# Layer 0 FFN: selecting the top 128 from quarters instead of halves, and narrow products in four column groups

## The chip, the cores and the metric

The kernel runs on one core of a Trainium2 chip. The metric is the time of one execution on the device in microseconds (us), from the first to the last instruction and what lies around them; of several runs the median counts. A profile of one execution gives the start and duration of each instruction on each engine: TensorE (PE; its weight loads PEld), VectorE (DVE), ScalarE (ACT), GpSimd (POOL) and SyncE (SP).

## What is computed

The reference is a network of four layers over x of 4 x 512 x 128 float32 values. Each layer is a feed-forward part (FFN), an attention and the same FFN again, each added to x. The change touches the FFN of layer 0 alone, which runs twice, before and after layer 0's attention:

```
def _L0_ffn_ref(x, input_patterns, process_input_weights, process_values, output_input_weights, output_patterns):
    k_input = max(n_input // 8, 64)        # 1024 // 8 = 128
    k_process = max(n_process // 8, 32)    # 512 // 8 = 64
    k_output = max(n_output // 8, 64)      # 1024 // 8 = 128
    input_acts = gelu(jnp.einsum('bsd,nd->bsn', x, input_patterns))
    input_acts_seq = input_acts.mean(axis=1)
    top_input_acts, top_input_idx = jax.lax.top_k(input_acts_seq, k_input)
    brow = jnp.arange(B)[:, None]
    input_repr = jnp.zeros((B, n_input), x.dtype).at[brow, top_input_idx].set(top_input_acts)
    process_acts = gelu(jnp.einsum('bn,pn->bp', input_repr, process_input_weights))
    top_process_acts, top_process_idx = jax.lax.top_k(process_acts, k_process)
    selected_process_values = process_values[top_process_idx]
    process_weights = jax.nn.softmax(top_process_acts, axis=-1)
    aggregated_value = jnp.einsum('bk,bkd->bd', process_weights, selected_process_values)
    output_acts_seq = gelu(jnp.einsum('bd,od->bo', aggregated_value, output_input_weights))
    top_output_acts, top_output_idx = jax.lax.top_k(output_acts_seq, k_output)
    selected_output_patterns = output_patterns[top_output_idx]
    out_per_seq = jnp.einsum('bk,bkm->bm', top_output_acts, selected_output_patterns)
    return jnp.broadcast_to(out_per_seq[:, None, :], (B, S, d_model))
```

The caller adds half of it: `x = x + 0.5 * _L0_ffn_ref(_layernorm(x), ...)`. There are four sequences, so each selection takes the 128 largest of 1024 numbers for each of four rows.

## The kernel before, in words

All of x stays in SBUF, and so do the weights of layer 0 (tile `w0`, one column block for each matrix) and the constants (tile `cst`, among them `selb`, four matrices of which the b-th copies row b to all 128 partitions). The layers follow one another. Inside a stage a scheduler orders the instructions of each engine, but for those that `mm_in_order` and `transpose_in_order` pin to the program's order. Engines wait for one another by semaphores. Products are recorded in the profile under the lines of their helpers: `mm` is L158, `transpose` L161, `mm_in_order` L164; they are told apart by the tiles that they write.

`l0_ffn` (from L329, called at L1822 and L1824) works in this order, and each step needs the one before:

1. For each of four sequences, eight products of input patterns with the normalized x (tile `pa`), each followed by a Gelu on ScalarE that also sums over the positions, into one column of `acc` (L346). POOL sets `acc` and `agg` to zero at the start (L334), because only 4 of 32 columns are used.
2. `acc` is turned by four transposes into rows, `ra`: 64 partitions of 512, the first half of the 1024 numbers on partitions 0 to 3, the second on 32 to 35. VectorE scales one half (L407), ScalarE the other (L408). `vals` is the same by neuron (L410).
3. `largest` finds the 128th largest number of each row. It runs 16 rounds on both halves at once. MAX8 (L365) takes the eight largest of each partition in falling order; MATCH_REPLACE8 (L367, with a short load of the eight values) writes a very low number over them. So each half gets a list of 128 in falling order. One list is read backwards (L370), and the maximum of the two lists position by position (L371) holds the 128 largest of both; their minimum (L373) is the limit. The limit is spread over the partitions by a small transpose (L374 to L378), and comparisons with `vals`, with a rule for ties by place (L380 to L399), give the numbers that are kept, all others zero (L401).
4. These, 128 x 4 in each of eight chunks, are the stationary side of eight products with `piw` that add up in one bank, `pp` (4 partitions x 512), then Gelu (L418).
5. The top 64 of 512 on four partitions (L424 and L425), softmax (L429 to L434), transposes (`pt_w`) and products (`pg`) to `agg` (L444).
6. Two products with `oiw` write the output row in two halves of 512 (`po0`), each followed by a Gelu into `oa` (L450). `by_neuron` transposes `oa` (L354), and `largest` runs again, on `oa`.
7. Eight products with `op` add up in `po1` (4 x 128), VectorE copies them to `o4` (L457), four products with `selb` spread row b over all partitions (`pb`), and four VectorE operations add to x (L464).

A float32 product is two instructions (passes) on TensorE. PSUM has banks with the tags "s" (4), "t" (2) and "m" (2). After the second call the tile of `w0` is loaded with the weights of layer 3 (L1826).

Of the kernel before, what the change touches and what calls it, by code (L numbers as in the profile page):

```python
# [103 lines left out]
def tile_macaron(ctx, tc, x_in, const_in, vec_in, w0_in, ws_in, ws3_in, w2f_in, w3_in, out):  # L104
# [223 lines left out]

    def l0_ffn(tag):  # L329
        with pool(tag) as sb:  # L330
            acc = sb.tile([P, 4, 2, 32], F32, name="acc")
            agg = sb.tile([64, 32], F32, name="agg")
            for padded in (acc, agg):
                nc.gpsimd.memset(padded, 0.0)  # L334
            ra = sb.tile([64, 512], F32, name="ra")
            oa = sb.tile([64, 512], F32, name="oa")
            halves = (slice(0, 32), slice(32, 64))
            finish_chains()
            ip = W0(w0, "ip")
            for b in range(B):  # L340
                begin_sequence(b, True)
                for c in range(8):
# [3 lines left out]
                    nc.scalar.activation(ga, pa, AF.Gelu, accum_out=acc[:, c % 4, c // 4, b : b + 1])  # L346

            def by_neuron(row, name):
# [3 lines left out]
                for c in range(4):  # L352
                    transpose(pt[:, ts(c, 64)], row[:, ts(c, P)])
                nc.vector.tensor_copy(  # L354
                    r.rearrange("p (h c) b -> p c h b", h=2), pt[:, :256].rearrange("p (c h b) -> p c h b", c=4, h=2)[:, :, :, :B]
# [3 lines left out]
            def largest(row, vals, name):  # L359

                w = sb.tile([64, 512], F32, tag="w512", name=f"w_{name}")
                order = sb.tile([64, P], F32, tag="order", name="order")
                for i in range(P // 8):
                    m8, src = order[:, ts(i, 8)], w if i else row
                    nc.vector.max(m8, src)  # L365
                    if i < P // 8 - 1:
                        nc.vector.match_replace(w, m8, src, GONE)  # L367
                turned = sb.tile([B, P], F32, tag="turned", name="turned")
                a = order[32 : 32 + B, P - 1 : P]
                nc.vector.tensor_copy(turned, bass.AP(a.tensor, a.offset, [list(a.ap[0]), [-1, P]]))  # L370
                nc.vector.tensor_tensor(turned, turned, order[:B, :], ALU.max)  # L371
# [28 lines left out]
                r = sb.tile([P, 8, B], F32, tag="kept", name=name, bufs=2)  # L400
                nc.vector.tensor_mul(r, above, vals)  # L401
                return r

            pt = bank("t", "pt_a")
            for c in range(4):
                transpose(pt[:64, ts(c, P)], acc[:, c, :, :].rearrange("p h b -> p (h b)"))
            nc.vector.tensor_scalar_mul(ra[halves[0]], pt[halves[0]], 1.0 / S)  # L407
            nc.scalar.activation(ra[halves[1]], pt[halves[1]], AF.Copy, scale=1.0 / S)  # L408
# [45 lines left out]
            for c in range(8):  # L454
                mm(po[:B, :D], oT[:, c, :], op[:, c, :], c == 0, c == 7)
# [1537 lines left out]
```

## Time and profile before

| What | Value |
|---|---|
| Median of three runs | 2940.64 us |
| Lowest and highest | 2930.02 and 2940.65 us |
| The profiled execution's own time | 2936.27 us |
| Its span, first to last instruction | 2934.6 us |
| Mean granted TensorE clock | 0.864 |
| First call of `l0_ffn`, up to its last addition to x | 0 to 144.3 us |
| Second call, from the normalization to its last addition | 287.7 to 417.1 us |
| DVE busy in 48 to 142 us | 65.1 of 94.0 us |
| DVE busy in 320 to 415 us | 65.4 of 95.0 us |

In a row of the timeline stand the start and the duration in us, the engine, the line, the operation, the tile written and the tiles read, partitions x elements of each, and how many are merged in that row; brackets hold the idle time before it and what ended that. In a table of stretches each engine's busy us stand with the number of its instructions in parentheses, then the granted TensorE clock, the share of DMA and its GB/s.

### The profile page before, as it was taken

Reading aid. Unit: us, or ns where it says so; the run is one execution under the profiler, and the core shown is the slowest. Engines: PE = TensorE matmul, PEld = TensorE weight load, DVE = VectorE, ACT = ScalarE, POOL = GpSimd, SP = SyncE. Lnnn points to the kernel's source line nnn. Section 1 sums busy time; section 2 is a strip of 40 time slices with the busy share of each in tenths; the row PEclk is TensorE's granted clock in tenths of the full one; section 3 lists DMA queues with packets and bytes.
Section 4 is the critical chain, followed back from the end, with each engine's and each line's share of the span. In section 5 each row is a group of like instructions: output and inputs, shape, how many; then the busy total and the mean of one; then the engine's idle time right before and its main releaser. Section 6 shows DMA issues by size and latency. Waiting matters only on the chain.

```text
span 2934.6 us, 46900 instructions
## 1 busy us (share of the span) xinstructions
PE 2274.4 (78%) x17558; PEld 1179.6 (40%) x17558; DVE 1808.6 (62%) x4776; ACT 1246.5 (42%) x2682; POOL 913.9 (31%) x1700
## 2 busy tenths in 40 slices
PE   4277528888678998958577678988689999689987
PEld 2145213333333333338456545555322222355553
DVE  4656476676576676454564477777356564777763
ACT  3044303433332433314232266776224444467763
POOL 1012012332122222202322387775200000677661
PEclk8588758999887999768777789999779999899998
DMA  3042010000000000008105410000000000100000
GB/s 133 0 152 81 0 58 1 1 1 1 1 1 1 1 1 4 4 7 290 36 13 189 143 30 21 21 21 12 1 1 1 1 1 1 26 23 19 21 21 11
DMA packets 33771, 99.12 MB, mean 34 GB/s; under 512 B 6184, under 2 KB 12072, under 8 KB 33032
## 3 DMA queue, kind: packets, MB, share of 16 engines
q1 hardware_dynamic: 30616, 88.03, 9.2%
q0 software_dynamic: 2496, 5.12, 0.8%
q8 instruction: 138, 2.26, 0.3%
q10 hardware_dynamic: 432, 2.98, 0.3%
q14 instruction: 89, 0.73, 0.1%
HBM read 66.88 MB, written 14.55 MB: 28 GB/s over the span
## 4 chain that ended last, share of the span: by engine, by line
PE 51%; DVE 22%; ACT 10%; POOL 9%; issue 6%; DMA 2%; SPq 0%; POOLq 0%; DVEq 0%; ACTq 0%
PE pk_at L164 10%; PE po_at L164 6%; ACT PT L787 4%; PE pa L164 3%; PE pag L164 3%; PE po L164 3%; PE pe L164 3%; PE p_qk L164 2%; POOL t L1603 2%; PE pg L164 2%; DVE t L1599 2%; PE pv L164 2%; DVE t L1596 2%; DVE y L997 2%; PE pq_at L164 2%
## 5 line engine op out<-in xcount | busy, mean ns | idle before, releaser
L787 ACT ACTIVATE PT<-pk_at 128x1024 f32<-128x1024 f32 (+3 forms) x384 | 311.1, 810 | 554.6 <-PE pq_at L164 478.1
L164 PE MATMUL pk_at<-qx,km 32*128 32x512 f32 (+3 forms) x1536 | 372.2, 562 | 62.3 <-ACT PT L787 57.3
L164 PE MATMUL po_at<-PT,vh 128*32 128x512 f32 (+3 forms) x1536 | 335.1, 519 | 3.1 <-POOL PT L790 2.8
L757 DVE CUSTOM_DVE_ANT_0 s<-pq_at,cst 128x384 f32<-128x384 f32 (+3 forms) x512 | 248.6, 485 | 100.8 <-PE pq_at L164 89.5
L1548 ACT ACTIVATE s<-s,nm,rn 128x128 f32<-128x128 f32 x512 | 245.5, 482 | 2.3 <-DVE nm L1654 2.0
L790 POOL TENSOR_SCALAR_AFFINE_SELECT PT<-PT 128x256 f32<-128x256 f32 x256 | 107.6, 422 | 422.9 <-ACT PT L787 422.8
L164 PE MATMUL pq_at<-km,qT 32*128 32x384 f32 (+3 forms) x1024 | 225.9, 530 | 14.1 <-DVE nm L757 7.7
L164 PEld LDWEIGHTS pk_at<-qx,km 32*128 32x128 f32 x1536 | 121.0, 191 | 271.9 <-ACT PT L787 209.0
L752 DVE TENSOR_REDUCE nm<-pq_at 128x2 f32<-128x1024 f32 x128 | 156.2, 1225 | 104.8 <-PE pq_at L164 104.0
L1603 POOL TENSOR_TENSOR t<-t,t 128x1024 f32<-128x1024 f32 x64 | 151.5, 2367 | 134.7 <-DVE t L1599 134.4
L161 PE MATMUL pt_y<-ident,y 128*128 128x128 f32 x224 | 54.6, 375 | 156.9 <-DVE y L214 117.9
L164 PE MATMUL pq_at<-km,t 32*128 32x512 f32 x512 | 149.6, 690 | 7.0 <-DVE nm L752 4.8
L164 PE MATMUL p_qk<-w,hT 128*128 128x512 f32 x256 | 144.0, 691 | 10.8 <-DVE t L1599 9.0
L164 PEld LDWEIGHTS po_at<-PT,vh 128*32 128x32 f32 x1536 | 56.0, 110 | 222.7 <-issue 148.2
L161 PE MATMUL pt<-ident,s 128*128 128x128 f32 x640 | 93.3, 293 | 65.4 <-POOL s L1666 40.4
L241 ACT COPY yT<-pt_y 128x512 f32<-128x512 f32 x56 | 32.8, 585 | 258.1 <-PE pt_y L161 258.1
L1666 POOL TENSOR_TENSOR s<-s,sm 128x1024 f32<-128x1024 f32 x64 | 121.5, 1898 | 49.1 <-DVE sm L1665 41.0
L1596 DVE TENSOR_TENSOR t<-p_qk,w 128x1024 f32<-128x1024 f32 x64 | 78.3, 1223 | 71.4 <-ACT sq L1548 71.1
L1548 ACT ACTIVATE sq<-p_qk 128x1024 f32<-128x1024 f32 x64 | 65.6, 1024 | 128.3 <-PE p_qk L164 72.7
L161 PEld LDWEIGHTS pt<-ident,s 128*128 128x128 f32 x640 | 78.6, 151 | 97.6 <-POOL s L1666 51.3
L161 PEld LDWEIGHTS pt_y<-ident,y 128*128 128x128 f32 x224 | 34.6, 171 | 188.1 <-issue 112.1
L1290 DVE SCALAR_TENSOR_TENSOR hT<-pa,w,sg 128x128 f32<-128x128 f32 x184 | 51.8, 345 | 85.1 <-ACT sg L1289 64.0
(424 smaller groups left out, 5197.0 us busy)
## 6 DMA issues: line engine op xcount, KB each, us to landing
w<-in_w2f_dram SPq DMA_DIRECT2D x46, 836.0 KB, 5.8
vb<-v SPq DMA_DIRECT2D x112, 128.0 KB, 2.2
skew<-qe SPq DMA_DIRECT2D x16, 512.0 KB, 3.0
rel<-skew SPq DMA_DIRECT2D x64, 128.0 KB, 3.5
w<-in_w_dram SPq DMA_DIRECT2D x1, 4147.0 KB, 12.4
w<-in_w_dram SPq DMA_DIRECT2D x1, 3200.0 KB
od<-o SPq DMA_DIRECT2D x46, 64.0 KB, 4.9
yd<-y SPq DMA_DIRECT2D x8, 256.0 KB, 2.3
```

Source lines behind the costliest of these rows:

```text
L161: return nc.tensor.transpose(dst, src, ident[: src.shape[0], : src.shape[0]])
L164: tc.keep_in_program_order(nc.tensor.matmul(dst, lhsT=lhsT, rhs=rhs, start=start, stop=stop))
L752: nc.vector.tensor_reduce(to, pq.rearrange("p (i n) -> p i n", i=2), AX.X, ALU.max)
L757: nc.vector.tensor_tensor_reduce(s[:, :nk], pq[:, i * 512 : i * 512 + nk], causal[:, S - nk :], 1.0, -BIG, ALU.add, ALU.max, nm[:, qt, at ...
L787: by_order(nc.scalar.activation(PT[:, :, q0:], pk[:, :, q0:], AF.Exp, scale=SC8))
L790: nc.gpsimd.affine_select(d, d, pattern=[[0, 2], [1, P]], base=0, channel_multiplier=-1, compare_op=ALU.is_ge, fill=0.0)
L997: nc.vector.scalar_tensor_tensor(yt, pe[e // 4][:, ts(e % 4, D)], st["g"][:, t, e : e + 1], yt, ALU.mult, ALU.add)
L1548: tc.keep_in_program_order(nc.scalar.activation(*args, **kw))
L1596: nc.vector.tensor_mul(by_head(t1), by_head(p3), over(tab[:, 0]))
L1599: nc.vector.tensor_mul(by_head(t2[:, :, a]), by_head(p3[:, :, z]), over(tab[:, 1, :, a]))
L1603: nc.gpsimd.tensor_add(t1, t1, t2)
L1666: nc.gpsimd.tensor_mul(s, s, bcast(sm, P))
```

## The change

`largest` works on quarters. `acc` is laid out so that two full transposes give 128 partitions of 256: quarter q of sequence b on partition 32 q + b. The 16 rounds run on 128 x 256. After them lie four sorted lists of 128 for each sequence. A new helper, `larger`, does what L370 and L371 did: one list read backwards, and the maximum with the other. It is called first for 64 partitions (quarters 2 and 3 against 0 and 1). What it leaves are the 128 largest of each pair, no longer in falling order but rising and falling at most once, so seven stages of maximum and minimum over halves, quarters and so on put them in order again, between two tiles `two`. Then `larger` is called for four rows, as before.

The result goes into one of two tiles `kept`, 32 columns a chunk of which four are used, zeroed once on POOL. In the products with `piw` and `op` chunk c goes to the 32-partition strip c % 4 of PSUM: four strips with two chunks each. For `piw` the strips are copied to SBUF in two parts and added by one product with the first columns of `selb`, which now has its ones in all four strips; for `op` the four products with `selb` add them. The output row is four products of 256 columns, one a strip, and one Gelu of 128 x 256. No load is added; the constant has the same size.

The diff, cut to its core:

```diff
@@ -326,15 +326,18 @@
     def l0_ffn(tag):
         with pool(tag) as sb:
-            acc = sb.tile([P, 4, 2, 32], F32, name="acc")
+            acc = sb.tile([P, 2, 4, 32], F32, name="acc")
             agg = sb.tile([64, 32], F32, name="agg")
-            for padded in (acc, agg):
+            kept = [sb.tile([P, 8, 32], F32, name=f"kept{i}") for i in range(2)]
+            for padded in (acc, agg, *kept):
                 nc.gpsimd.memset(padded, 0.0)
-            ra = sb.tile([64, 512], F32, name="ra")
-            oa = sb.tile([64, 512], F32, name="oa")
-            halves = (slice(0, 32), slice(32, 64))
+            ra = sb.tile([P, 256], F32, name="ra")
+            oa = sb.tile([P, 256], F32, name="oa")
+            selb = const("selb")
             finish_chains()
             ip = W0(w0, "ip")
             for b in range(B):
@@ -343,32 +346,43 @@
                     pa = bank("s", "pa")
                     mm_in_order(pa, ip[:, ts(c, P)], yT[:, b, :])
                     ga = sb.tile([P, S], F32, tag="ga", name="ga", bufs=2)
-                    nc.scalar.activation(ga, pa, AF.Gelu, accum_out=acc[:, c % 4, c // 4, b : b + 1])
+                    nc.scalar.activation(ga, pa, AF.Gelu, accum_out=acc[:, c % 2, c // 2, b : b + 1])
 
             def by_neuron(row, name):
 
                 r = sb.tile([P, 8, B], F32, tag="by_n", name=name, bufs=2)
                 pt = bank("t", "pt_c")
-                for c in range(4):
-                    transpose(pt[:, ts(c, 64)], row[:, ts(c, P)])
+                for c in range(2):
+                    transpose(pt[:, ts(c, P)], row[:, ts(c, P)])
                 nc.vector.tensor_copy(
-                    r.rearrange("p (h c) b -> p c h b", h=2), pt[:, :256].rearrange("p (c h b) -> p c h b", c=4, h=2)[:, :, :, :B]
+                    r.rearrange("p (q c) b -> p c q b", q=4),
+                    pt[:, :256].rearrange("p (c q b) -> p c q b", c=2, q=4)[:, :, :, :B],
                 )
                 return r
 
-            def largest(row, vals, name):
-
-                w = sb.tile([64, 512], F32, tag="w512", name=f"w_{name}")
-                order = sb.tile([64, P], F32, tag="order", name="order")
+            def larger(dst, lists, n, at):
+
+                a = lists[at : at + n, P - 1 : P]
+                nc.vector.tensor_copy(dst, bass.AP(a.tensor, a.offset, [list(a.ap[0]), [-1, P]]))
+                nc.vector.tensor_tensor(dst, dst, lists[:n, :], ALU.max)
+
+            def largest(row, vals, r):
+
+                w = sb.tile([P, 256], F32, tag="w256", name="w256")
+                order = sb.tile([P, P], F32, tag="order", name="order")
                 for i in range(P // 8):
                     m8, src = order[:, ts(i, 8)], w if i else row
                     nc.vector.max(m8, src)
                     if i < P // 8 - 1:
                         nc.vector.match_replace(w, m8, src, GONE)
+                two = [sb.tile([64, P], F32, tag=f"two{i}", name="two") for i in range(2)]
+                larger(two[0], order, 64, 64)
+                for i in range(7):
+                    halves = [t.rearrange("p (n i k) -> p n i k", i=2, k=64 >> i) for t in (two[i % 2], two[1 - i % 2])]
+                    for to, op in enumerate((ALU.max, ALU.min)):
+                        nc.vector.tensor_tensor(halves[1][:, :, to, :], halves[0][:, :, 0, :], halves[0][:, :, 1, :], op)
                 turned = sb.tile([B, P], F32, tag="turned", name="turned")
-                a = order[32 : 32 + B, P - 1 : P]
-                nc.vector.tensor_copy(turned, bass.AP(a.tensor, a.offset, [list(a.ap[0]), [-1, P]]))
-                nc.vector.tensor_tensor(turned, turned, order[:B, :], ALU.max)
+                larger(turned, two[1], B, 32)
                 limit = sb.tile([B, 1], F32, tag="limit", name="limit")
                 nc.vector.tensor_reduce(limit, turned, AX.X, ALU.min)
                 nc.vector.tensor_copy(turned, limit.to_broadcast([B, P]))
@@ -397,23 +411,25 @@
                     equal, place[:, : 8 * B].rearrange("p (c b) -> p c b", b=B), float(P), equal, ALU.is_le, ALU.mult
                 )
                 nc.vector.tensor_add(above, above, equal)
-                r = sb.tile([P, 8, B], F32, tag="kept", name=name, bufs=2)
-                nc.vector.tensor_mul(r, above, vals)
-                return r
+                nc.vector.tensor_mul(r[:, :, :B], above, vals)
 
             pt = bank("t", "pt_a")
-            for c in range(4):
-                transpose(pt[:64, ts(c, P)], acc[:, c, :, :].rearrange("p h b -> p (h b)"))
-            nc.vector.tensor_scalar_mul(ra[halves[0]], pt[halves[0]], 1.0 / S)
-            nc.scalar.activation(ra[halves[1]], pt[halves[1]], AF.Copy, scale=1.0 / S)
+            for c in range(2):
+                transpose(pt[:, ts(c, P)], acc[:, c, :, :].rearrange("p q b -> p (q b)"))
+            nc.vector.tensor_scalar_mul(ra, pt[:, :256], 1.0 / S)
             vals = sb.tile([P, 8, B], F32, tag="by_n", name="vals", bufs=2)
-            nc.vector.tensor_scalar_mul(vals.rearrange("p (h c) b -> p c h b", h=2), acc[:, :, :, :B], 1.0 / S)
-            reprT = largest(ra, vals, "reprT")
-
-            pp = bank("m", "pp")
+            nc.vector.tensor_scalar_mul(vals.rearrange("p (q c) b -> p c q b", q=4), acc[:, :, :, :B], 1.0 / S)
+            largest(ra, vals, kept[0])
+
+            p4 = bank("m", "pp4")
             piw = W0(w0, "piw").rearrange("p (c n) -> p c n", n=512)
             for c in range(8):
-                mm(pp[:B, :], reprT[:, c, :], piw[:, c, :], c == 0, c == 7)
+                mm(p4[ts(c % 4, 32), :], kept[0][:, c, :], piw[:, c, :], c < 4, c >= 4)
+            pq = sb.tile([P, 512], F32, name="pq4")
+            nc.vector.tensor_copy(pq[:, 0:256], p4[:, 0:256])
+            nc.vector.tensor_copy(pq[:, 256:512], p4[:, 256:512])
+            pp = bank("m", "pp")
+            mm(pp[:B, :], selb.rearrange("p (b n) -> p b n", n=P)[:, :, 0], pq)
             pa = sb.tile([B, 512], F32, name="pact")
             nc.scalar.activation(pa, pp[:B, :], AF.Gelu)
 
@@ -444,21 +460,20 @@
             nc.vector.tensor_copy(agg[:, :B], pg[:64, :B])
 
             oiw = W0(w0, "oiw")
-            for half, at in enumerate(halves):
-                po = bank("m", "po0")
-                mm(po[at, :], agg, oiw[:64, ts(half, 512)])
-                nc.scalar.activation(oa[at], po[at, :], AF.Gelu)
-            oT = largest(oa, by_neuron(oa, "out"), "oT")
+            po = bank("m", "po0")
+            for q in range(4):
+                mm(po[ts(q, 32), :256], agg, oiw[:64, ts(q, 256)])
+            nc.scalar.activation(oa, po[:, :256], AF.Gelu)
+            largest(oa, by_neuron(oa, "out"), kept[1])
             po = bank("m", "po1")
             op = W0(w0, "op").rearrange("p (c n) -> p c n", n=D)
             for c in range(8):
-                mm(po[:B, :D], oT[:, c, :], op[:, c, :], c == 0, c == 7)
-            o4 = sb.tile([B, D], F32, name="o4")
-            nc.vector.tensor_copy(o4, po[:B, :D])
+                mm(po[ts(c % 4, 32), :D], kept[1][:, c, :], op[:, c, :], c < 4, c >= 4)
+            o4 = sb.tile([P, D], F32, name="o4")
+            nc.vector.tensor_copy(o4, po[:, :D])
             pb = bank("m", "pb")
-            selb = const("selb")
             for b in range(B):
-                mm(pb[:, ts(b, D)], selb[:B, ts(b, P)], o4)
+                mm(pb[:, ts(b, D)], selb[:, ts(b, P)], o4)
             for b in range(B):
                 xb = x[:, ts(b, TB), :]
                 nc.vector.scalar_tensor_tensor(xb, rows(pb[:, ts(b, D)], TB), 0.5, xb, ALU.mult, ALU.add)
@@ -1861,8 +1876,8 @@
     f8 = np.arange(128) // HD
     m3 = np.where(k128 < 64, k128 >= i64, k128 - 64 <= i64)
     m3f = m3 & ((p[:, None] >= 64) | (k128 >= 64))
-    selb = np.zeros((B, B, P), f)
-    selb[np.arange(B), np.arange(B), :] = 1.0
+    selb = np.zeros((4, 32, B, P), f)
+    selb[:, np.arange(B), np.arange(B), :] = 1.0
     perm = np.zeros((P, P), f)
     perm[p, p ^ 1] = 1.0
     return CONST.pack({
@@ -1877,7 +1892,7 @@
         "pm4": (p[:, None] // 32 == f8[None, :] % 4).astype(f),
         "perm": perm, "kmask": ((p[:, None] % 32) // HD == np.arange(4)[None, :]).astype(f),
         "kmax": -((p[:, None] % 32) == HD * (np.arange(4)[None, :] ^ 1)).astype(f),
-        "rev": np.broadcast_to(8.0 - np.arange(8), (P, 8)), "selb": selb,
+        "rev": np.broadcast_to(8.0 - np.arange(8), (P, 8)), "selb": selb.reshape(P, B * P),
         "iota": np.broadcast_to(np.arange(128), (P, 128)), "row1": p[:, None] * NT + np.arange(NT)[None, :] + 1,
         "lower8": np.broadcast_to(np.tri(8, 8, -1)[None], (P, 8, 8)),
     })
```

## The prediction

> **What bounds the kernel now.** I read the page first, for the span and the chain of work that ended last.
>
> ```profile
> span 2934.6 us, 46900 instructions
> PE 2274.4 (78%) x17558; PEld 1179.6 (40%) x17558; DVE 1808.6 (62%) x4776; ACT 1246.5 (42%) x2682; POOL 913.9 (31%) x1700
> ...
> PE 51%; DVE 22%; ACT 10%; POOL 9%; issue 6%; DMA 2%; SPq 0%; POOLq 0%; DVEq 0%; ACTq 0%
> ```
>
> TensorE bounds the kernel as a whole, but this is an average over stages. The change touches two stages only, the two calls of the layer 0 FFN (some 0 to 144 and 290 to 417 us), so I then asked for the busy time in the four stretches in which `largest` takes its top 128.
>
> ```profile
> core 0: us, PE busy (x) PEld busy (x) DVE busy (x) ACT busy (x) POOL busy (x), PEclk, DMA share, GB/s
> 51.17:74.42 23.25, 0.00 (x0) 0.00 (x0) 22.16 (x47) 0.00 (x0) 0.00 (x0) 0.53 0.00 0
> 107.70:131.08 23.38, 0.68 (x4) 0.50 (x4) 22.25 (x48) 0.00 (x1) 0.00 (x0) 0.50 0.00 0
> 323.54:346.80 23.26, 0.00 (x0) 0.00 (x0) 22.16 (x47) 0.00 (x0) 0.00 (x0) 0.54 0.00 0
> 380.40:403.81 23.41, 0.68 (x4) 0.50 (x4) 22.26 (x48) 0.04 (x1) 0.00 (x0) 0.50 0.00 0
> ```
>
> VectorE is busy for 22.2 of each 23.3 us, and nothing else works. These 93.3 us are a chain on one engine: what is saved there comes off the end. The timeline shows one round of that chain, a few of the narrow operations behind it, and how narrow products behave in another stage.
>
> ```profile
> 52.70 0.69 DVE L365 MAX8 order<-w_reprT 64x8 f32<-64x512 f32 x1
> 53.42 0.08 DVE L367 MATCH_VALUE_LOAD w_reprT<-order,w_reprT 64x8 f32 x1
> 53.50 0.67 DVE L367 MATCH_REPLACE8 w_reprT<-order,w_reprT 64x512 f32<-64x512 f32 x1
> 54.20 0.69 DVE L365 MAX8 order<-w_reprT 64x8 f32<-64x512 f32 x1
> ...
> 74.42 0.21 DVE L370 COPY turned<-order 4x128 f32<-4x128 f32 x1
> 74.67 0.28 DVE L371 TENSOR_TENSOR turned<-turned,order 4x128 f32<-4x128 f32 x1
> 74.98 0.27 DVE L373 TENSOR_REDUCE limit<-turned 4x1 f32<-4x128 f32 x1
> ...
> 76.06 0.19 DVE L380 TENSOR_TENSOR equal<-vals,lim 128x32 f32<-128x32 f32 x1
> 76.17 0.18 DVE L381 TENSOR_TENSOR above<-vals,lim 128x32 f32<-128x32 f32 x1
> ```
>
> ```profile
> 801.82 1.81 PE L164 MATMUL po_1a<-PT,vm 128*32 128x128 f32 x32
> ```
>
> A round is 1.50 us (52.70 to 54.20). L380 and L381 don't depend on each other and start 0.11 us apart; dependent ones (L371 to L373) start one duration plus 0.03 us apart.
>
> [...] The po_1a row agrees: its four column groups start within 0.02 us of each other, and 32 instructions take 1.81 us where the single-file product of the same width (po at 135.81, 16 instructions) takes 3.58. [...] product pp starts its passes 0.85 us apart, and 0.43 us from its seventh on, after 4.1 us. [...]
>
> **The change part by part, for one call of l0_ffn.**
>
> *Preparing the first row (L407, L408).* VectorE 32x512 in 0.68 us, then ScalarE 0.59 after it: 49.86 to 51.20, 1.34 us. After: one 128x256. [...] 0.68 - 0.27 = 0.41, and 0.03 to the next. The last transpose loads 128 columns where it loaded 64, +0.05. Sum **-0.85**.
>
> *Selection rounds, twice.* Each takes 16 MAX8 (0.686) and 15 MATCH_REPLACE8 (0.667), 31 passes over 512 elements; now over 256. The trace has no other width of these two. [...] 31 x 0.267 x 2 = **-16.5**. From 64 to 128 partitions costs nothing that shows: 4 rows took 0.68 (L424), 64 rows 0.69. Bounds: 0 (all fixed) to -16.5.
>
> *The added merge, twice.* A copy and a maximum on 64 partitions, priced by L370 and L371: 0.25 + 0.31. Then seven stages of maximum and minimum over 64 elements: [...] ([...] I take 0.22). The two of a stage are independent: the second starts its duration less 0.08 after the first (L381: 0.18, and 0.11 later, with 0.18 - 0.08 = 0.10), so 0.14; the next stage needs both: 0.14 + 0.22 + 0.03 = 0.39. 7 x 0.39 = 2.73, with the first two 3.29, twice **+6.6**. Bounds for the seven stages: 2.0 if nothing ever waits (14 x 0.14), 4.0 if all is serial (14 x 0.25) [...]. All of it is on the path; nothing else is queued on VectorE.
>
> *Product pp (L158).* Before: 16 passes, 79.13 to ScalarE's start at 88.18, 9.05 us; 9.37 in the second call. After: eight products in four groups, thus four batches of one cold pass: 4 x 0.855 + 0.2 of drain = 3.62; two 128x256 copies out of PSUM at 0.41, the second overlapped, 0.74; one product pp of two passes, still cold, 0.855 + 1.06 = 1.91; three hand-overs of 0.04. Sum 6.4: **-2.8**. Bounds: -4.5 (last product warm) to +2.8 (groups in turn).
>
> *The output row (L450).* Before: two products (104.58) whose passes already go side by side, 1.92 us, then two ScalarE 32x512, to VectorE's start at 107.73: 3.15. After: two batches of 256-column passes, 2 x 0.43 + 0.2 = 1.06; one 128x256 activation 0.38 (row PT<-pk_at of that form); hand-overs 0.06. Sum 1.5: **-1.65**.
>
> *by_neuron (L354).* Two full transposes for four. They stay beside the first MAX8, but that is now 0.42 long, less than two cold transposes (some 0.65), so VectorE waits: **+0.2**.
>
> *Product po1 (L158).* 135.81 to 139.42, 3.61; after 4 x 0.213 + 0.2 = 1.1: **-2.5**. The copy o4 (0.28 at 4 partitions, L407 shows the same price per element at 32) and the four broadcast products (2.07) stay; these pay for columns, not rows.
>
> *At nothing:* two memsets of `kept` on POOL, 0.3 us each. POOL is idle from 9.5 to 13.4 us and in the second call has only L1333's memsets (288.48) behind it, which a much later stage wants; without that cover 0.6 us. The `selb` constant fills rows that were zero, same bytes. The large load of w3 (L1826) waits for product po1 and moves earlier with it, its users as well. No DMA is added.
>
> Sum: -0.85 - 16.5 + 6.6 - 2.8 - 1.65 + 0.2 - 2.5 = -17.5; two calls **-35 us**. The profiled execution took 2936.3 us (span 2934.6 and 1.7 around it): 2901.3. It lies 4.4 under the median 2940.6 of runs that spread over 10.6; from the median it would be 2905.6. I take the middle, **2903**.
>
> **Rivals.**
>
> 1. *Column groups go in turn* here, since two passes of one group are issued back to back. Against my values pp costs +5.6, the output row +2.5, po1 +2.5, a call 10.6: 2903 + 21 = **2924**, still faster by 0.56%. Against it: po_1a is also float32 with two passes and has its four groups start together.
> 2. *The rounds don't depend on width.* Then the 33 us of them stay: **2936**, no change. For it: no row shows another width. [...]
> 3. *Slower: a lower granted TensorE clock later.* If the clock were a budget that the idle stretches refill, 35 us less rest would be paid in the attention stages. TensorE is 51% of the chain, 1497 us: from 2.3% less clock on it takes back all 35 us, and at 4% (60 us) the result is **2963**. Against it: the clock right behind the first rest is 0.77 (142 to 200 us) and 0.93 in 2500 to 2934, where there is no rest before; rests cost clock, they don't store it.
>
> **How the numbers follow.** Forecast 0.87, rival 1 0.06, rival 2 0.05, rival 3 0.02. The forecast's own range: merge -3 to +5 over four, pp -3 to +7 (groups only two at a time), the runs' spread 5 either way; together some 2891 to 2920, which leaves out no more than 2 in 10. About 0.5% (14.7 us, the line at 2926) is what a measurement of this kernel can tell from no change. Faster by more: 0.93 (forecast and rival 1); within 0.05; slower 0.02.
>
> **What would show it.** MAX8 near 0.42 and MATCH_REPLACE8 near 0.40, 128x256, rounds of 0.97 us; the merge from the last MAX8 to the copy into `turned` 3.3 us; pp4 with four starts together and 3.6 us long; po1 1.1 us; each call 17 to 18 us shorter, and all from the first attention on the same but earlier. I am wrong if MAX8 stays above 0.6, if a merge takes over 6 us, or if a later stage grows by over 10 us.

## The result and the profile after

The changed kernel takes **2892.8 us** (median of four runs, 2886.26 to 2894.83) against 2936.6 for the kernel before (the three runs above and a fourth of 2932.45). The ratio is **0.9845, with a 95% interval of 0.9828 to 0.9863**: 1.5% faster, 43.8 us. The profiled execution of the changed kernel took 2886.3 us, 50.0 less than that of before.

The page's first lines, after:

```profile
span 2884.6 us, 46981 instructions
PE 2245.8 (78%) x17562; PEld 1171.8 (41%) x17562; DVE 1788.8 (62%) x4844; ACT 1243.1 (43%) x2678; POOL 911.9 (32%) x1704
```

The shares hardly move, because the change concerns two stages of some 75 us. So here are the four stretches of the selection rounds again, with the same columns as in the prediction:

```profile
core 0: us, PE busy (x) PEld busy (x) DVE busy (x) ACT busy (x) POOL busy (x), PEclk, DMA share, GB/s
50.78:66.03 15.25, 0.00 (x0) 0.00 (x0) 14.14 (x47) 0.00 (x0) 0.00 (x0) 0.60 0.00 0
97.54:113.17 15.63, 0.69 (x2) 0.29 (x2) 14.24 (x48) 0.00 (x0) 0.00 (x0) 0.50 0.00 0
309.66:324.90 15.24, 0.00 (x0) 0.00 (x0) 14.15 (x47) 0.00 (x0) 0.00 (x0) 0.61 0.00 0
356.40:372.10 15.70, 0.69 (x2) 0.29 (x2) 14.26 (x48) 0.05 (x1) 0.00 (x0) 0.50 0.00 0
```

The same 47 or 48 instructions of VectorE now take 15.2 to 15.7 us where they took 23.3 to 23.4. The two narrow products pp and po1 (tile `po`) of the first call, before:

```profile
79.13 9.01 PE L158 MATMUL pp<-w,reprT 128*4 128x512 f32 x16 [0.78 <-PE place L158]
...
135.81 3.58 PE L158 MATMUL po<-w,oT 128*4 128x128 f32 x16 [0.73 <-DVE oT L401]
```

After, the timeline of the first call shows one round, the end of the rounds with the merge behind it, and the narrow products:

```profile
51.80 0.43 DVE L375 MAX8 order<-w 128x8 f32<-128x256 f32 x1
52.26 0.09 DVE L377 MATCH_VALUE_LOAD w<-order,w 128x8 f32 x1
52.34 0.41 DVE L377 MATCH_REPLACE8 w<-order,w 128x256 f32<-128x256 f32 x1
52.78 0.43 DVE L375 MAX8 order<-w 128x8 f32<-128x256 f32 x1
...
66.03 0.22 DVE L366 COPY two<-order 64x128 f32<-64x128 f32 x1
66.28 0.28 DVE L367 TENSOR_TENSOR two<-two,order 64x128 f32<-64x128 f32 x1
66.60 2.68 DVE L383 TENSOR_TENSOR two<-two 64x64 f32<-64x64 f32 x14
69.31 0.21 DVE L366 COPY turned<-two 4x128 f32<-4x128 f32 x1
...
74.10 3.62 PE L158 MATMUL pp<-w,kept 128*32 128x512 f32 x16 [0.85 <-PE place L158]
77.79 0.42 DVE L429 COPY pq<-pp 128x256 f32<-128x256 f32 x1 [3.79 <-PE pp L158]
78.13 0.41 DVE L430 COPY pq<-pp 128x256 f32<-128x256 f32 x1
78.69 1.02 PE L158 MATMUL pp<-pq,cst 128*4 128x512 f32 x2 [0.96 <-DVE pq L430]
...
97.16 0.38 ACT L466 ACTIVATE oa<-po 128x256 f32<-128x256 f32 x1 [11.88 <-PE po L158]
...
121.34 1.08 PE L158 MATMUL po<-w,kept 128*32 128x128 f32 x16 [0.90 <-DVE kept L414]
```

A round is 0.98 us (51.80 to 52.78) instead of 1.50. The merge runs from 66.03 to 69.31: 3.28. The 16 passes of pp are one row of 3.62 us, four of them beside each other. The granted clock in both traces is either 0.50 or 1.00, half and full clock below, cold and warm in the prediction: in before the passes of pp that start 0.85 us apart lie at 0.50, those 0.43 apart at 1.00, from 83.15 us on. Step by step, each from the start of one row to the start of the next step's:

| Step | Predicted, a call | First call | Second call |
|---|---|---|---|
| Preparing the first row | -0.85 | -0.88 | -0.88 |
| Rounds, both selections (with by_neuron) | -16.5 + 0.2 | -8.00 - 7.75 | -8.00 - 7.75 |
| Merges added, both | +6.6 | +3.28 + 3.27 | +3.29 + 3.29 |
| Product pp to the Gelu's start | -2.8 | -3.40 | -3.71 |
| The output row | -1.65 | -1.60 | -1.59 |
| Product po1 | -2.5 | -2.47 | -2.47 |
| Small hand-overs | 0 | +0.2 | +0.1 |
| One call, from `vals` (L410, now L421) to the start of the additions to x (L464, now L479) | **-17.5** | **92.28 to 74.90: -17.4** | **92.66 to 74.97: -17.7** |

The two calls give back **35.1 us, where 35 were forecast**. But the profiles differ by 50 and the medians by 44. The rest lies in stages that nobody touched: from the first call's additions to `vals` of the second, with layer 0's attention in it, 180.1 us became 184.0; and from the second call's additions to the end 2520.0 became 2500.7 (the later part, below). There every engine issues the same instructions in the same order in both kernels, but for some ten of TensorE's 15346 passes. What differs is the granted clock. The largest piece in these two profiles is a stretch of layer 1 with the same 85 instructions of TensorE. The rows are of before, of after, and of a further profile of the unedited changed kernel (after_2, run 9):

```profile
core 0: us, PE busy (x) PEld busy (x) DVE busy (x) ACT busy (x) POOL busy (x), PEclk, DMA share, GB/s
1223.61:1250.20 26.59, 25.98 (x85) 8.85 (x86) 3.87 (x16) 5.84 (x10) 3.27 (x8) 0.50 0.00 1
1186.19:1205.46 19.27, 18.66 (x85) 6.62 (x86) 3.66 (x16) 5.84 (x10) 3.25 (x8) 0.73 0.00 1
1188.26:1213.90 25.64, 24.80 (x85) 8.62 (x86) 3.86 (x16) 5.84 (x10) 3.26 (x8) 0.54 0.00 1
```

From before to after it is 7.3 us less, at a granted clock (PEclk) of 0.73 instead of 0.50. The third row warns that this piece doesn't belong to the changed kernel as such: of its four profiles below, two have the 0.73, and the other two 0.54. The experiments thus had two questions: do the steps hold one by one, and where do the 9 us of the medians beyond them, the surplus below, come from?

### The profile page after: what moved, and what is told of

It reads as the page before. It is cut to its first block, busy times and chain, and to the rows that moved or that the text cites. A ratio compares the mean times of both kernels' runs of the same rounds, so it can differ in the third digit from the quotient of the medians.

```text
span 2884.6 us, 46981 instructions
## 1 busy us (share of the span) xinstructions
PE 2245.8 (78%) x17562; PEld 1171.8 (41%) x17562; DVE 1788.8 (62%) x4844; ACT 1243.1 (43%) x2678; POOL 911.9 (32%) x1704
## 5 line engine op out<-in xcount | busy, mean ns | idle before, releaser
L164 PE MATMUL po_at<-PT,vh 128*32 128x512 f32 (+3 forms) x1536 | 328.7, 510 | 4.4 <-POOL PT L805 4.2
```

Of the source, the lines that this page charges most:

```text
L164: tc.keep_in_program_order(nc.tensor.matmul(dst, lhsT=lhsT, rhs=rhs, start=start, stop=stop))
```

## Experiments

Two theories about the surplus stood from the first run on. **A: it is chance**, a matter of where the clock's changes fell in the few runs measured; only the direct 35 us belong to the change. **B: it lasts**, because the later stages start earlier. In the profiles the clock changed only at points 3.413 us apart (below); the time from one of them to the next is what the expectations call a clock window. Each run below is compared with runs of the kernel before on the same chip: medians 2940.75 (13 runs) for the first four, 2937.63 (27 runs) for the next four, 2937.48 (9 runs) for the last four. What the two calls take is read from one profile of each kernel, counted as in the table above. Two profiles of the kernel before differ in it by 0.7 us.

**1. The quarters without the column groups** (label quarters_alone). The products as before, in one strip; po1 likewise, and o4 on four partitions:

```diff
-                mm(p4[ts(c % 4, 32), :], kept[0][:, c, :], piw[:, c, :], c < 4, c >= 4)
...
-            nc.vector.tensor_copy(pq[:, 0:256], p4[:, 0:256])
-            nc.vector.tensor_copy(pq[:, 256:512], p4[:, 256:512])
...
-            mm(pp[:B, :], selb.rearrange("p (b n) -> p b n", n=P)[:, :, 0], pq)
+                mm(pp[:B, :], kept[0][:, c, :B], piw[:, c, :], c == 0, c == 7)
```

> The change without its column groups: products pp and po1 as before, one after another into one strip. From the two traces the direct parts of a call are then -0.9 (first row), -8.0 and -7.8 (rounds), +3.3 and +3.3 (merges), -1.6 (output row), together -11.5; two calls -23 us. Theory A (the further 10 us of the whole change are chance[...]): -23, give or take 6, with nothing lasting in later stages. Theory B (a shorter FFN shifts the later stages so that they are cold for less time, in every execution): -23 and some 7 more, about -30.

Measured: 2912.7 us (2908.83 to 2922.51), ratio 0.9914 (0.9888 to 0.994); 28.1 less than before. The interval, 17.6 to 32.9 less, holds A's number and B's. The two calls take 81.54 and 79.69 us, 23.7 less.

**2. The column groups without the quarters** (groups_alone). The kernel before, with its halves, and these lines for pp (po1 in strips likewise):

```diff
-                mm(pp[:B, :], reprT[:, c, :], piw[:, c, :], c == 0, c == 7)
+                mm(p4[ts(c % 4, 32), :], kept[0][:, c, :], piw[:, c, :], c < 4, c >= 4)
...
+            mm(pp[:B, :], selb.rearrange("p (b n) -> p b n", n=P)[:, :, 0], pq)
```

> The kernel before with the column groups alone: halves, 16 rounds of 64x512, but pp and po1 in four strips, with the two copies and the adding product for pp. Direct: pp -2.7 (last product cold) to -3.4 (warm), po1 -2.5 a call; two calls -10.4 to -11.8 us. Theory A: -11, give or take 6. Theory B: -11 and 3 more. If the groups went in turn it would be +6.

Measured: 2921.8 us (2915.77 to 2928.13), ratio 0.9938 (0.9918 to 0.9959); 19.0 less (12.1 to 24.1). That is past A's range of 5 to 17; B's 14 lies in the interval. The calls take 86.51 and 87.41, 11.0 less. The direct gains of the two parts add up: 23.7 + 11.0 = 34.7, of 35.1. Neither is needed for the other.

**3. As much time saved, in another way** (eleven_rounds). The kernel before with fewer rounds in both selections:

```diff
-                for i in range(P // 8):
+                nc.gpsimd.memset(order, 0.0)
+                for i in range(11):
...
-                    if i < P // 8 - 1:
+                    if i < 10:
```

> The kernel before with 11 of the 16 selection rounds in each of the four selections (the lists have 88 values, the rest is zero, so the limit is not the 128th largest). No product changes. Direct: 4 x 5 x 1.50 = -30 us. Theory A: -30, give or take 6. Theory B: about -39, since only the shortening matters to it.

Measured: 2906.7 us (2904.2 to 2913.08), ratio 0.989 (0.9866 to 0.9915); 34.1 less (25.0 to 39.4), and the calls 31.1 less. The surplus is 3: A's number, with B's 39 at the edge of the interval. That an FFN is merely shorter doesn't seem to bring the rest.

**4. The changed kernel again** (after_again), with no edit.

> The changed kernel once more, beside the kernel before on the same chip. Theory A: the difference of the medians moves towards the direct -34 (within -28 to -42), and the profiled execution's later part, from the second call's last addition to x to the end, differs from the 2501 us of the first profile by several us with another phase of the clock window. Theory B: -44 again, and the same cold stretches at the same places.

Measured: 2896.3 us (2883.7 to 2905.37), ratio 0.9847 (0.9818 to 0.9876); 44.5 less (36.5 to 53.5), of which the calls 35.2. So the surplus of 9 came back: B's number, though the interval reaches into A's range of 28 to 42. Taken together runs 1 to 4 fit neither theory well: groups_alone, 11 us shorter, had a surplus of 8, and eleven_rounds, 31 us shorter, one of 3.

**5 and 6. A small delay added, in both kernels** (after_late and before_late). Behind the copy to `o4`, in the second call alone, a chain of seven further copies. It is meant to move everything that follows by some 2 us, and is the only edit:

```diff
+            if tag == "l0g":
+                for i in range(7):
+                    late = sb.tile([P, D], F32, name=f"late{i}")
+                    nc.vector.tensor_copy(late, o4)
+                    o4 = late
```

> The changed kernel with seven more copies of o4, one after another, in its second call: all later stages start some 1.7 to 2.2 us later [...] and nothing else changes. Theory A (where the clock window falls in an execution is chance, the average of the later stages is the same for every kernel): the median is 1.7 to 2.2 us above the changed kernel's, 2896, give or take 4. Theory B (the later stages gained because of how far they moved): a half window undoes it, the median rises by 5 to 12, to 2900 or more.

Measured: 2905.5 us (2901.64 to 2915.35), ratio 0.9895 (0.9875 to 0.9916). That is 9.3 above the 2896.3 of run 4, and the mean of its six runs, 2906.7, is 11.7 above that of all 15 runs of the changed kernel, for a delay of 1.8 us in the second call (76.75 against 74.97). This is what B expected.

> The kernel before with seven such copies (4 x 128), 1.7 us. Theory A: its median rises by 1.7, give or take 4, to 2942. Theory B: it falls by several us, to 2936 or less, since a half window moves it to where the changed kernel is.

Measured: 2941.2 us (2935.12 to 2950.54, 22 runs), ratio 1.0012 (1.0004 to 1.0021); 3.5 more than before (1.2 to 6.2), for a delay of 1.8 (94.46 against 92.66). This is what A expected; B, by which it would fall, failed here. So the same delay costs some 9 to 12 us in one kernel and 1 to 6 in the other. Set against the profile of after, instruction by instruction, the profile of after_late is 1.6 us late at 480 us, 7.6 at 1000 and 17.7 at 1240, with the same instructions in nearly the same order: the lateness grows in steps. Not all of it is the delay's, for that profile of after is the fastest of four. Counted from the second call's additions, after_2 and after_again, with no edit, are themselves some 10 us behind it at 1260 us, and after_late is 7.7 and 7.8 behind these two there.

**7. Without the sort between the two merges** (no_sort):

```diff
-                for i in range(7):
-                    halves = [t.rearrange("p (n i k) -> p n i k", i=2, k=64 >> i) for t in (two[i % 2], two[1 - i % 2])]
-                    for to, op in enumerate((ALU.max, ALU.min)):
-                        nc.vector.tensor_tensor(halves[1][:, :, to, :], halves[0][:, :, 0, :], halves[0][:, :, 1, :], op)
...
-                larger(turned, two[1], B, 32)
+                larger(turned, two[0], B, 32)
```

> The changed kernel without the seven stages that put the lists in order (so the second merge works on lists out of order and the limit is not the 128th largest). It measures what the order costs: the trace has 2.68 us for the 14 operations, four times 2.7 with the hand-over: -10.8 us against the changed kernel, 2883. If more or less than that moves beyond 5 us, it comes from the clock window of later stages, as theories A (chance) or B (always) say.

Measured: 2889.3 us (2886.78 to 2894.41), ratio 0.9839 (0.9819 to 0.9858). The calls take 70.33 and 69.39, 10.2 less than with the sort; four blocks of 2.7 are 10.8. So nearly all that the sort costs is on the path. The whole lies 6.9 below run 4, and not at the 2883 expected: some 3 us of what the calls give were lost again in stages that were not touched.

**8. TensorE kept at full clock through the selections** (keep_warm). Behind each MAX8, and in two places of the merge, an unread product of eight columns:

```diff
+                warm, busy = bank("s", "warm"), W0(w0, "piw")[:, :512]
...
                     nc.vector.max(m8, src)
+                    mm(warm[:8, :], m8, busy)
...
+                mm(warm[:8, :], two[0][:, :8], busy[:64])
...
+                    if i == 2:
+                        mm(warm[:8, :], two[1][:, :8], busy[:64])
```

and in the top 64 of step 5 the same with the four rows there.

> The changed kernel with products that nobody reads, 8 columns of an order or m8 tile against 512 columns of weights, one behind each MAX8 of the three selections of a call and two behind the merges, so that TensorE is busy while VectorE selects. Nothing on VectorE changes. If activity holds the clock up through these stretches: pp4 3.6 to 1.9 us, pb 2.1 to 1.0, the output row and po1 0.4 each, the start of the following stage 1 to 3, some 4 to 7 a call, 8 to 14 us less, 2882 to 2888; this beats both kernels. If products of 8 columns don't count as activity, or those of the top 64 (4 rows) don't: 0 to -4. If they get in the way of the products that matter: up to +4.

Measured: 2916.3 us (2911.84 to 2920.53), ratio 0.993 (0.9912 to 0.9947): some 20 us slower than the changed kernel, where the forecasts went from 14 less to 4 more. The calls take 79.79 and 79.84, 4.9 more each; the other half is lost in stages that were not touched. Its timeline:

```profile
67.19 0.99 DVE L386 TENSOR_TENSOR two<-two 64x64 f32<-64x64 f32 x5 [0.86 <-PE warm L158]
68.77 1.13 DVE L386 TENSOR_TENSOR two<-two 64x64 f32<-64x64 f32 x6 [0.59 <-PE warm L158]
...
82.58 13.82 PE L158 MATMUL warm<-w,m 4*8 4x512 f32 x16 [1.39 <-DVE m L446]
...
100.72 16.00 PE L158 MATMUL warm<-w,order 128*8 128x512 f32 x32
```

The brackets of the first two rows show the larger part of the 4.9: VectorE waits 0.86 and 0.59 us for a product that reads `two` before it may write there again, in each of two merges. In the first call another 0.95 goes to four waits in the top 64 for the products that read `m`, and 0.84 to the last product pp, which is at half clock again (1.86 us). The third row shows why the top 64 got nothing for it either. Its 16 passes on four rows follow each other at 0.86 us, where a pass of 512 columns at full clock has 0.43. They are 13.82 us long and stay at half clock to the end, though TensorE is busy throughout; the passes on 128 rows below it run at full clock from 2.4 us after their start. At 120.2, ahead of po1, the full clock was gone again.

**9 to 11. Both kernels once more** (after_2; after_3 and before_2 with one run each), with no edit.

> The changed kernel a third time, to see whether its later stages lie low in every session. Take R as an execution's time less the two calls of the FFN from their first row to their last addition: 2754 for the kernel before, 2744 for the ten timed runs of the changed kernel, 2749 to 2755 for six edits of the two. Theory A (chance): R of these six runs lies near 2752 and the median near 2902. Theory B (a lasting property of this length of the FFN): R again 2744, the median 2894.

> One more profile of the changed kernel. The place of the clock windows relative to the end of the first call was 0.22 and 0.43 us in its two profiles, with 183.9 us from there to the second call both times; the kernel before had 2.73 and 180.1. Theory A: any place from 0 to 3.4, and the stretch follows it (184 at 0.2 to 0.5, 182.3 near 1.5, 180 near 2.6). Theory B: again 0.2 to 0.4 and 184, and the part after the second call 2501 to 2511.

> One more profile of the kernel before. Theory A: another place of the windows and the stretch from the first to the second call by the same curve, 180 to 184; the later part anywhere from 2501 to 2520. Theory B: 2.5 to 2.7 and 180 again, the later part 2520.

Measured: 2899.6 us (2897.39 to 2900.75), ratio 0.9867 (0.9845 to 0.9888), 37.9 less than before; 2889.2; and 2935.8. In after_2 the surplus is 2.8, and R is 2750, between the two theories. From the second call's additions on after_2 took 2514.0 us, after_3 2503.6, before_2 2513.5. After_3 came as B has it (place 0.01 us, 183.7 us to the second call). Before_2 came as A has it: another place, 3.15, and 183.3.

**12. Full clock for the tail alone** (warm_tail): the products of run 8 from the eighth MAX8 on, four behind the last, one ahead of each place product, none in the top 64 and none that reads `two`.

```diff
                     nc.vector.max(m8, src)
+                    for _ in range(4 if i == 15 else i > 6):
+                        mm(warm[:8, :], m8, busy)
...
+                mm(warm[:8, :], order[:, 120:128], busy)
...
+                mm(warm[:8, :256], order[:, 120:128], busy[:, :256])
```

> The changed kernel with unread products of 8 columns, 128 rows deep, only behind the last nine MAX8 of each top-128 selection, four behind the last and one each ahead of the two products of place; none reads a tile that VectorE writes again soon. If they bring TensorE to full clock and hold it: pp4 3.6 to 1.9, po1 1.1 to 0.7, pb 2.1 to 1.1, 3 to 4 us a call, 6 to 8 in all, median 2886 to 2890. If the merge's 3 to 5 thin us let the clock fall again: 0. If the unread products are late and hold up pt_l: up to +4.

Measured: 2892.5 us (2882.79 to 2897.88), ratio 0.9841 (0.9817 to 0.9865). The calls take 72.45 and 72.52, 4.9 less in all than the changed kernel. In the timeline the two grouped products are nearly halved, as po1 shows:

```profile
118.74 0.64 PE L158 MATMUL po<-w,kept 128*32 128x128 f32 x16 [0.90 <-DVE kept L419]
```

po1 takes 0.64 us for 1.08, and pp's four groups 1.92 for 3.62. The whole is 7 below after_2 beside it, but only 3 below the mean of all 15 runs of the changed kernel (2895.0). The 4.9 us in the FFN are shown; that the whole kernel keeps them is not. In the FFN 6 to 8 were expected. Most of the difference is that full clock didn't last to the end of the call: the products pb, expected at 1.1 us, took 1.93 after 2.08. It ended although TensorE was not idle: it was busy for 1.94 and 2.04 us of the last 3.41 at full clock, in keep_warm and in warm_tail:

```profile
core 0: us, PE busy (x) PEld busy (x) DVE busy (x) ACT busy (x) POOL busy (x), PEclk, DMA share, GB/s
116.76:120.17 3.41, 1.94 (x4) 0.09 (x2) 1.82 (x11) 0.00 (x0) 0.00 (x0) 1.00 0.00 0
116.59:120.00 3.41, 2.04 (x23) 1.15 (x24) 1.59 (x10) 0.00 (x0) 0.00 (x0) 1.00 0.00 0
```

**All runs side by side.** The surplus is what the whole moved less what the two calls moved. With four to eight runs that scatter by some 5 us a median is good to about 3, and most 95% intervals reach 5 to 9 us either way, so no single surplus of this table is clear of chance by much.

| Kernel | Whole, against before | The two calls | Surplus |
|---|---|---|---|
| after; again; _2 | -43.8; -44.5; -37.9 | -35.1; -35.2; -35.1 | -8.7; -9.3; -2.8 |
| after_late | -32.1 | -32.4 | +0.3 |
| quarters_alone | -28.1 | -23.7 | -4.4 |
| groups_alone | -19.0 | -11.0 | -8.0 |
| eleven_rounds | -34.1 | -31.1 | -3.0 |
| before_late | +3.5 | +1.6 | +1.9 |
| no_sort | -48.3 | -45.2 | -3.1 |
| keep_warm | -21.3 | -25.3 | +4.0 |
| warm_tail | -45.0 | -40.0 | -5.0 |

The surplus doesn't grow with the time that the calls save. And chance alone is a poor account: 54 runs of before have a mean of 2938.6 and 15 of after one of 2895.0, which is 43.6 apart (give or take 3), not 35.

**What the surplus consists of.** In each of the 14 profiles the clock changes only at multiples of 3.413 us from one another, a grid whose start differs from run to run (the places below, 0.01 to 3.15 us in the first call). In before the trace records 138 stretches of one clock and in after 132, and each starts within 0.01 us of such a multiple. How much of the later part passes at half clock (cold, below) differs, 545 to 581 us, and so does its time, 2501 to 2520. Less half its cold time it is 2225 to 2237 us in all 14, and the scatter (standard deviation) falls from 5.7 to 3.2 us: the clock accounts for much of it, and not for all. The two pure kernels and three others, with the place of the grid: the us from the start of a call's additions to the next point of the grid (worked out from the trace's record of clock changes):

| Profile | Place, first call | To the second call | Place, second call | Later part | Of it cold |
|---|---|---|---|---|---|
| before | 2.73 | 180.1 | 3.05 | 2520.0 | 581 |
| before_2 | 3.15 | 183.3 | 3.37 | 2513.5 | 561 |
| after | 0.43 | 184.0 | 0.91 | 2500.7 | 545 |
| after_again | 0.22 | 183.9 | 0.78 | 2510.8 | 558 |
| after_2 | 0.41 | 183.9 | 0.93 | 2514.0 | 579 |
| after_3 | 0.01 | 183.7 | 0.81 | 2503.6 | 548 |
| after_late | 1.65 | 182.5 | 1.82 | 2518.7 | 580 |
| quarters_alone | 2.58 | 180.0 | 2.34 | 2515.8 | 571 |
| eleven_rounds | 1.62 | 182.3 | 1.67 | 2515.1 | 568 |

The third column follows the second closely: places from 2.46 to 2.73 give about 180.0 us, 1.45 to 1.65 give 182.2 to 182.5, 0.01 to 0.54 give 183.7 to 184.2, and the one of 3.15 gave 183.3, over all 14 profiles. So the 3.9 us that the first pair of profiles differ by in this stretch go with the grid's place, and not with the kernel: before_2, at 3.15, took 183.3 as well.

The same record shows that this stretch pulls the work into step with the grid. The places behind the first call lie anywhere from 0.01 to 3.15 us, but `vals` of the second call starts either 2.62 to 2.75 us after a point of the grid (the six profiles with places of 0.01 to 0.54 or 3.15) or 3.21 to 3.35 us after one (the eight with 1.45 to 2.73). From there the length of the second call fixes the place at its end. This is why the four profiles of after, all of the first kind, lie within 0.15 us of one place there. Which kind it is, the kernel alone doesn't fix: after_late has the changed kernel's first call without an edit, and yet its profile had the place 1.65 and was of the second kind. So its profile differed ahead of the delay, and that all four of after were of one kind may be luck in part.

For the later part the rule is loose: from one place within 0.15 us the four profiles of after spread from 2500.7 to 2514.0. Their mean, 2507.3, is 9.5 below that of the two profiles of before.

What stands: the changed kernel's runs lie 8 us below what its two calls give back, and a delay of 1.8 us in the second call takes that away (run 5, in the times of its six runs). In the profiles the later work lies otherwise against the clock's grid, and three of the four of after have the shortest later part of all 14. That the place of the grid is the cause of the surplus is not shown: groups_alone had a surplus of 8 in its median, and its one profile the place 1.50, like after_late and eleven_rounds, which had none or 3. Of the variants only one run each was profiled. Open also is why the later part still spreads from one place. Delays in finer steps, which would draw the curve, weren't tried.

## Why the prediction was right, and where it was not

2903 was forecast with a range of 2891 to 2920; 2892.8 was measured, inside the range near its low end. **The mechanism and the sum of the steps were right**. Of the 10 us between, 1.4 come from the start of the sum (2938, the middle between a profile and a median, where 2936.6 was measured), and nearly 9 from a statement beside the sum.

- *Rounds.* Their time does go with the elements: MAX8 took 428 ns for 256 elements after 686 for 512, MATCH_REPLACE8 408 after 667. The forecast took 267 off each for 256 elements less. That was an estimate from other operations of before, 0.28 us at 128 elements and 0.68 at 512, thus 1.04 ns an element; the measured steps are 258 and 259. The first row's 128 x 256 (L419) took 0.42 where the same estimate gave 0.41. The two selections of a call gave -15.75 against -16.5 + 0.2; the smaller steps alone explain some 0.5 of that. MATCH_VALUE_LOAD rose from 83 to 92 ns and the by_neuron transposes (0.69 us for the two) hold the second selection's first rounds somewhat longer than the 0.2 that I gave them (15.60 us against 15.22).
- *Merge.* 3.28 against 3.29. The 14 operations of the seven stages took 2.68 us as one row, forecast 2.73: a pair overlaps, a stage waits for the pair before. One took 214 ns (207 to 219 in all 56) where the forecast had 0.22 us; by the same 1.04 ns an element, 0.28 us for 128 give an estimate of 0.21. The short runs of the later stages cost nothing that shows. Of the forecast's upper bound of 4.0 only 14 x 0.25 = 3.5 goes back to the trace. Run 7 shows that nearly all of it lies on the path (10.2 us of 10.8).
- *Column groups.* pp's four groups together 3.62 us (9.01 before), as forecast; po1 1.08 (1.1; 3.58 before); the output row -1.6 (-1.65). Run 2 shows these parts alone at -11.0 for two calls; worked out, 2 x (2.8 + 2.5) = 10.6. What was to stay did: the copy o4 took 0.29 us on 128 partitions after 0.28 on four, the four products pb 2.08 over 128 rows after 2.07 over four.
- *Mis-sized: the last product pp.* I held it at half clock and gave it 1.91 us. It took 1.02, at full clock: in the first call the granted clock went from 0.50 to 1.00 at 77.58 us, 3.48 us after the grouped passes began, and the product started at 78.69. The prediction's own bound (-4.5) allowed for it. Hence -3.4 and -3.7 in place of -2.8, some 1.5 us in two calls. It offsets the 0.5 us a call that the rounds fell short. So it is partly luck that the sum holds within 0.2 us; its steps hold within 1.
- *Wrong: "all from the first attention on the same but earlier".* The order of the instructions is the same, their times are not. To the second call the stretch grew by 3.9 us in the profile (by 0.7 against before_2), the later part shrank by 19.3 (by 9.5 between the means of the profiles of each kernel). I had allowed 5 us either way for the runs' spread, and nothing for a difference in later stages that most runs of one kernel share; it is 8 us here, and its cause stays open. That the result stayed inside the range owes something to the widths given to the merge and to pp, which were meant for other things.
- *Rivals.* Groups in turn (2924): refuted by the one row of 3.62 us for 16 passes. Rounds that don't depend on width (2936): refuted by 428 ns. A lower clock later (2963): the later part passed 545 to 579 us at half clock in the four profiles of after and 561 and 581 in the two of before, and no later stage is longer by 10 us.

## What to carry to other kernels

Read a chain on one engine as instructions x (fixed part + elements per partition): when the other partitions are free, halving the elements (here MAX8 from 686 ns on 64 x 512 to 428 on 128 x 256) and paying a merge of small operations (3.28 us) is easily priced from rows of the trace, and the sum held here within 0.2 us of 35. But a change of some 1% in a kernel whose TensorE clock moves up and down (0.50 or 1.00, in 138 stretches of the profile of before) can have a second term: later stages that nobody touched take another time. Here it was worth 8 us in the mean of the changed kernel's 15 runs, nearly a quarter of the direct gain, and between -9 and +4 in the medians of single sessions and variants. So compare the changed stages from their own first to last row before crediting a change with the whole difference, and try the change with a small delay added.

## What the runs showed of the hardware

- In keep_warm being busy was not enough for TensorE's full clock: passes with four rows, back to back for 13.8 us, stayed at half clock (0.86 us for each pass of 512 columns), while passes on 128 rows with eight output columns got it (0.43 us) after 2.4 us.
- Full clock was lost though TensorE had been busy for 1.94 of the last 3.41 us (at 120.2 us in keep_warm) and for 2.04 of them (at 120.0 in warm_tail).
- The clock changed only at points 3.413 us apart in all 14 profiles, and the stretch with layer 0's attention ended in one of two narrow places between such points, 2.62 to 2.75 or 3.21 to 3.35 us after one, wherever it began.
- With a delay of 1.8 us in one place the kernel was 9.3 us slower than in run 4. The same stretch of 85 products took 26.6 us at a clock of 0.50 and 19.3 at 0.73, the latter in two of four profiles of one kernel. The spread of the later part over the 14 profiles, 19.3 us of some 2900, is 0.7%, and yet is over half of what the change itself brings.
- Float32 products, two passes each, ran side by side in four column groups: the four groups started within 0.05 us of each other, and 16 passes of 512 columns took 3.62 us at half clock (after) and 1.92 at full clock (warm_tail).
